# Redistributing weight-lookup steps between two phases of a fused attention and FFN kernel

## The chip, the core and the metric

The kernel runs as one program on one core of a Trainium2 chip. The metric is the device time of one execution in microseconds (us); the time before is the median of three runs. Engines are named as the profile names them: PE (TensorE matmul), PEld (its weight load), DVE (VectorE), ACT (ScalarE), POOL (GpSimd) and SP (SyncE, which issues most of the DMAs). PSUM is the memory that PE writes; SBUF is the memory that the other operands live in.

## What is computed

The input x has 8 sequences of 1024 tokens with 512 features. Cut to what matters, the reference is:

```python
xn = layernorm(x)
# recurrent attention, three decays i
q = xn @ Wq;  gate = softmax(xn @ Wg)
k = xn @ Wk[i];  v = xn @ Wv[i]
w = sigmoid(decay_logits[i]) ** max(s - t - 1, 0) * (s > t)
blended += gate[..., i] * ((q @ k.T * w) @ v)
s = blended @ Wo * out_scale
# FFN whose weights are looked up: w = lut[idx], lut has 16 entries
gate_ = xn @ lut[gate_idx].T;  up = xn @ lut[up_idx].T
h = silu(gate_) * up                                   # 1376 wide
g = silu(h @ lut[down_idx].T)
out = x + s * g
```

The FFN weights are not given; they are built on the chip from integer indices (1376x512, twice, and 512x1376) and a table of 16 floats.

## The kernel before

**Two phases.** `phase_1` runs the attention for all eight sequences, writes the blended result and the layer-normed inputs to DRAM, and beside that builds the FFN weights. `phase_2` runs the FFN for all eight sequences with matmuls in Winograd's form (products 1 to 7 of a 2x2 block scheme, nested twice), and ends with the multiplication of both parts.

**Lookups.** `look_up` (L212) builds one tile of weights, 128x1024, on DVE as a generator. Between two `yield`s stands one DVE instruction: three bit masks (`bit`, L217), one shift (L220), then a binary tree of eight `leaf` selections (L224) joined by seven `copy_predicated` (L241). One such instruction is called a lookup step here. When a tile is done, POOL adds and subtracts blocks of it (L271 to L275), and after every second tile it builds the tile `pair` (L289, L291, L296, L299 for gate and up; L335, L337, L340, L342 for down). Results go to DRAM through SP: L287, L297 and L300 for gate and up, L334, L338 and L343 for down, and L278 for those tiles (o of 8, 9 and 10) that are also needed whole. Stores are not issued at once: `defer(n, ...)` issues them after n calls of `tick`.

**Phase 1's loop.** For each b of 0 to 8 and each k of 0 to 7 (L741 onwards) three generators are advanced: `project(b)` (layer norm, transposes, features), `chunks(b - 1)` (the recurrence, one chunk of 128 tokens for each k) and `weights`, the build of FFN weights. One pass over k is called a slot here; in the trace a slot runs from one `pr` (L662) to the next. How many steps of `weights` a slot takes stands in the tuple `steps`, three places in a slot. Four slots are called a half.

In a slot DVE does, beside lookups, `pr` (L662, the masked scores that PE needs for `po`, L684), `ga` (L637, gate times query, which PE needs for the next slot's scores `psc`, L660), in some slots the sums `ts` (L515, L519, L524, L530) for the feature products, and twice an addition to `qk` (L537, L540). POOL does `qb` (L641) and small pieces of the layer norm (L423, L424).

The gates go a long way. After the softmax (L462) SP writes them transposed to DRAM (`gTd`, L468), and then reads them back for all partitions (`ga<-gTd`, L483); that read waits for the write. DVE's L637 reads what came back. Each b has two such trips, one per 512 tokens.

**Order.** `keep_order` chains each of PE, DVE, ACT and POOL to the order in which the program text issues them. SP is chained in that way only up to b of 0, k of 3; after that the recording layer places SP's DMAs, and SP works through them in that order: a DMA that waits holds up all behind it on SP.

**Phase 2's nodes.** `quads` (L960) goes through 17 nodes for each b. In a node PE does seven products; DVE makes `t[1] = t[1] + e` (L920) and `t[3] = t[2] + e` (L924), and product 3 cannot start before L920. In nodes (1, 1) and (5, 5) the results leave PSUM through ACT, in others through DVE. For b of 0, `left_weights` (L355) is advanced beside the nodes: one more tile of lookups, whose result (`wdl`) is needed after the last node. The line that does it before is

```python
                    some(made, 4 if node.ks in ((1, 1), (5, 5)) else 1)   # L1084
```

It stands after `node.seventh()`, so its DVE instructions follow L924 of the node and precede L920 of the next.

Of the kernel before, what the change touches and what calls it, by code (L numbers as in the profile page):

```python
# [48 lines left out]
def recurrent_block(ctx: ExitStack, tc, x, wq, wk, wv, wo, wg, decay_logits, out_scale, lut, gidx, uidx, didx, out):  # L49
# [19 lines left out]
    nc = tc.nc  # L69
# [13 lines left out]
    NQ = NO // 4  # L83
# [49 lines left out]
    def defer(parts, issue):  # L133
        later.append([parts, issue])
# [111 lines left out]
    def ffn_weights(build, pool, pair_pool):  # L246

        upper = []

        def gate_up(o):
            s, m = OCH[o]
            n = 2 * NV * m
            idx = build.tile([P, NB], I32, name="idx", tag="idx", bufs=2)  # L260
            iv = idx[:, :n].rearrange("p (a b) -> p a b", b=m)
            gs, us = (src[:, s : s + m].rearrange("(c p) b -> p c b", p=P) for src in (gidx, uidx))
            nc.sync.dma_start(out=iv[:, 2:6, :], in_=gs)
            nc.sync.dma_start(out=iv[:, 0:2, :], in_=us[:, 0:2, :])
            nc.sync.dma_start(out=iv[:, 6:8, :], in_=us[:, 2:4, :])
            yield
            wf = pool.tile([P, 2 * NB], F32, name="wgu", tag="wgu", bufs=3)
            yield from look_up(build, wf[:, :n], idx[:, :n], P, n)
            w = wf[:, : 2 * n].rearrange("p (k two m) -> p k two m", two=2, m=m)
            a21, a11, a12, a22, s1, s2, s3, s4 = (w[:, k] for k in range(8))  # L270
            nc.gpsimd.tensor_tensor(s1, a21, a22, ALU.add)  # L271
            nc.gpsimd.tensor_tensor(s2, s1, a11, ALU.subtract)
            yield
            nc.gpsimd.tensor_tensor(s3, a11, a21, ALU.subtract)
            nc.gpsimd.tensor_tensor(s4, a12, s2, ALU.subtract)  # L275
            wide = wf[:, 2 * m : 2 * n].rearrange("p (a b) -> p a b", b=m)
            if o >= 4 * NQ:
                defer(3, lambda: nc.sync.dma_start(out=wgu_d[o], in_=wide))  # L278
            if o >= 2 * NK:
                return  # L280
            if o % 2 == 0:
                upper.append(w[:, 1:])
                return
            up, low = upper.pop(), w[:, 1:]
            to = quad_d[o // 4][:, :, o // 2 % 2, :].rearrange("p k (t m) -> p k t m", m=P)
            pair = pair_pool.tile([P, 7, 3, P], F32, name="pair", tag="pair")
            nc.sync.dma_start(out=to[:, :, 0:2, :], in_=up)  # L287
            b21, b22, b11, b12 = low[:, :, 0], low[:, :, 1], up[:, :, 0], up[:, :, 1]
            nc.gpsimd.tensor_tensor(pair[:, :, 0], b21, b22, ALU.add)  # L289
            yield  # L290
            nc.gpsimd.tensor_tensor(pair[:, :, 1], pair[:, :, 0], b11, ALU.subtract)  # L291
            yield
            if o >= 4 * NQ:
                for _ in range(4):
                    yield
            nc.gpsimd.tensor_tensor(b21, b11, b21, ALU.subtract)  # L296
            defer(3, lambda: nc.sync.dma_start(out=to[:, :, 2:4, :], in_=low))  # L297
            yield
            nc.gpsimd.tensor_tensor(pair[:, :, 2], b12, pair[:, :, 1], ALU.subtract)  # L299
            defer(4, lambda: nc.sync.dma_start(out=to[:, :, 4:7, :], in_=pair))  # L300
            for _ in range(3):
                yield

        def down_tail():
            s, m = OCH[-1]
            idx = build.tile([P, NB], I32, name="idx", tag="idx", bufs=2)
            nc.sync.dma_start(out=idx[:m, :V], in_=didx[s : s + m, :])
            yield
            wf = pool.tile([P, 2 * NB], F32, name="wgu", tag="wgu", bufs=3)
            yield from look_up(build, wf[:m, :V], idx[:m, :V], m, V)  # L310
            defer(2, lambda: nc.sync.dma_start(out=wdt_d, in_=wf[:m, :V]))

        def down(rows, e):
            idx = build.tile([P, NB], I32, name="idx", tag="idx", bufs=2)
            for a, row in enumerate(rows):
                nc.sync.dma_start(out=idx[:, ts(a, V)], in_=didx[ts(row, P), :])
            yield
            t = pool.tile([P, 2 * NB], F32, name="wgu", tag="wgu", bufs=3)
            yield from look_up(build, t[:, : 2 * V], idx, P, 2 * V)
            b11, b12, b21, b22, t1, t2, t4 = (t[:, ts(k, V // 2)] for k in range(7))  # L320
            nc.gpsimd.tensor_tensor(t1, b12, b11, ALU.subtract)
            nc.gpsimd.tensor_tensor(t2, b22, t1, ALU.subtract)
            yield
            nc.gpsimd.tensor_tensor(b12, b22, b12, ALU.subtract)
            nc.gpsimd.tensor_tensor(t4, b21, t2, ALU.subtract)
            halves = t[:, : 7 * V // 2].rearrange("p (k o m) -> p k o m", o=2, m=P)
            if len(upper) == 0:
                upper.append(halves)
                return
            up, low = upper.pop(), halves  # L330
            b11, b12, b21, b22 = up[:, :, 0], up[:, :, 1], low[:, :, 0], low[:, :, 1]
            pair = pair_pool.tile([P, 7, 3, P], F32, name="pair", tag="pair")
            to = wd_d[:, :, e, :].rearrange("p k (t m) -> p k t m", m=P)
            defer(3, lambda: nc.sync.dma_start(out=to[:, :, 2:4, :], in_=low))  # L334
            nc.gpsimd.tensor_tensor(pair[:, :, 0], b12, b11, ALU.subtract)  # L335
            yield
            nc.gpsimd.tensor_tensor(b12, b22, b12, ALU.subtract)  # L337
            defer(2, lambda: nc.sync.dma_start(out=to[:, :, 0:2, :], in_=up))  # L338
            yield
            nc.gpsimd.tensor_tensor(pair[:, :, 1], b22, pair[:, :, 0], ALU.subtract)  # L340
            yield
            nc.gpsimd.tensor_tensor(pair[:, :, 2], b21, pair[:, :, 1], ALU.subtract)  # L342
            defer(4, lambda: nc.sync.dma_start(out=to[:, :, 4:7, :], in_=pair))  # L343
            for _ in range(8):
                yield

        jobs = [gate_up(o) for o in range(NO)] + [down_tail()]
        jobs += [down((j, j + 4), j % 2) for j in (0, 2, 1, 3)]
        next(jobs[0])
        yield  # L350
        for job, following in zip(jobs, jobs[1:] + [iter(())]):
            next(following, None)
            yield from job
# [347 lines left out]
    def phase_1():  # L701
        nonlocal small, p_a, p_c, p_r
        with (
# [37 lines left out]
            for b in range(B + 1):  # L741
                following = project(b + 1, pools, sides, kept) if b + 1 < B else iter(())
                older = chunks(b - 1, (chk, blp), kept) if b else iter(())
                for k in range(NC):


                    if b == 0:
                        steps = (k > 0, k >= NC // 2, 2 * (k >= NC // 2))
                    elif b < B:
                        steps = ((1, 1, 4), (1, 2, 4), (1, 2, 4), (1, 2, 3))[k % 4]  # L750
                    else:
                        steps = (1, 0, 0)
                    tick()
                    next(newer, None)

                    for _ in range((0, 0, 0, 0, 0, 0, 1, 2)[k] if b == 0 else k >= NC - 3):
                        next(following, None)
                    next(older, None)
                    next(setup, None)
                    build_some(steps[0])  # L760
                    next(more, None)
                    tick()
                    if k < NC // 2:
                        for _ in range(2):
                            next(ending, None)
                    next(newer, None)
                    build_some(steps[1])
                    next(older, None)
                    build_some(steps[2])
                    if k < NC // 2:  # L770
                        next(ending, None)
                    tick()
                    next(newer, None)
                    next(older, None)
                    if (b, k) == (0, 3):
                        sums_of_weights(wqk_sb, wqs)
                        keep_order(tc, seen, (mybir.EngineType.SP,))
# [16 lines left out]
    def phase_2():  # L794
        with (
# [164 lines left out]
            def quads(b, xs, h, sums, made, at_last):  # L960
# [108 lines left out]
                node, empty, after = next(todo)  # L1069
# [3 lines left out]
                while empty:  # L1073
# [7 lines left out]
                    at_last(node.ks == (2, 3))  # L1081
                    node.seventh()
                    empty(node.t, 3)
                    some(made, 4 if node.ks in ((1, 1), (5, 5)) else 1)  # L1084
                    node.product(1, 3)
                    empty(node.t, 1)
                    at_last(node.ks in ((5, 7), (2, 3)))
                    if following:
                        following.fifth()
# [10 lines left out]
            def some(weights, n):  # L1100
                for _ in range(n):
                    next(weights, None)
# [363 lines left out]
```

## Time and profile before

| | |
|---|---|
| median of three runs | 2103.63 us (2103.54 to 2104.08) |
| the profiled execution, its own time | 2103.83 us |
| its span, first to last instruction | 2101.9 us |
| PE busy | 2086.2 us, 99% |
| DVE, ACT, POOL busy | 1441.4, 943.6, 1038.5 us |
| phase 1 (until the first FFN product) | 0 to 584 us |
| lookups and their POOL work in phase 1 | until 539 us |
| `left_weights` in phase 2 | 584 to 678 us |
| mean granted TensorE clock | 0.999 |

The profile is one execution. Its page has the busy time of each engine, the span in 40 slices, the chain of work that ended last, and the costliest groups of instructions; further views list who waited for whom, the instructions of one engine in order of time, and busy time by stretch. In a line of the timeline the first number is the start in us from the begin of the span, the second the time, then engine, line, operation, what it writes and reads, and the count; a bracket gives idle time just before it and what ended it. Two instructions on one line (x2, x3) share the time. PE's matmuls overlap, so PE is bound where the next one starts a fixed time after the last: 216 ns for 256 columns. Where the start comes later than that, PE stood still.

### The profile page before, as it was taken

The page shows a single profiled execution, that of the slowest core. Times are in us where ns is not written, and L with a number is a line of the kernel's source. Part 1 is how long each engine was busy: PE and PEld are TensorE (multiplying, and loading weights), DVE is VectorE, ACT ScalarE, POOL GpSimd, SP SyncE. Part 2 cuts the span into 40 slices and gives each one's busy share as a digit, 9 for nine tenths or more (in the row PEclk, how much of TensorE's full clock was granted, in tenths as well). Part 3 has the DMA queues.
Part 4 walks back from the last instruction along what each step waited for, and adds up shares of the span by engine and source line. Part 5 has one row for each costly group of instructions (what it writes and reads, how often), then busy time and mean ns, then how long its engine had stood idle before and what let it go on. Part 6 is the DMA issues. An engine that isn't in the chain of part 4 may idle for free.

```text
span 2101.9 us, 32181 instructions
## 1 busy us (share of the span) xinstructions
PE 2086.2 (99%) x11691; PEld 1751.8 (83%) x11691; DVE 1441.4 (69%) x2214; ACT 943.6 (45%) x2116; POOL 1038.5 (49%) x1050
## 2 busy tenths in 40 slices
PE   9999999999999999999999999999999999999999
PEld 7887888888878888797878888787988888797877
DVE  8889998879357775675567456656755665675567
ACT  4766676676344324423531542344144224424531
POOL 4554664364364456517443741664275265527432
PEclk9999999999999999999999999999999999999999
DMA  8766769654754734554454446345544634464442
GB/s 218 147 178 165 208 149 211 158 164 125 210 177 139 258 134 161 169 216 145 157 215 152 160 151 238 138 149 196 189 146 153 249 128 158 151 233 145 146 156 106
DMA packets 184347, 359.68 MB, mean 171 GB/s; under 512 B 50895, under 2 KB 122206, under 8 KB 184190
## 3 DMA queue, kind: packets, MB, share of 16 engines
q1 hardware_dynamic: 168742, 330.61, 50.4%
q10 hardware_dynamic: 10968, 12.34, 1.8%
q0 software_dynamic: 4480, 14.68, 1.7%
q8 instruction: 93, 1.52, 0.3%
q14 instruction: 64, 0.52, 0.1%
HBM read 281.95 MB, written 75.63 MB: 170 GB/s over the span
## 4 chain that ended last, share of the span: by engine, by line
PE 81%; DVE 2%; DMA 1%; issue 0%; POOL 0%; ACT 0%; SPq 0%; DVEq 0%; ACTq 0%
PE s L897 33%; PE sE L897 6%; PE s12d L1154 5%; PE s21d L1154 5%; PE s11d L1154 5%; PE fs L845 3%; PE pd L1272 3%; PE ps L1279 3%; PE pv L444 2%; PE sEd L1154 2%; PE po L684 2%; PE fsE L845 1%; PE s11d L1165 1%; PE s12d L1165 1%; PE s21d L1165 1%; PE sEd L1165 1%
## 5 line engine op out<-in xcount | busy, mean ns | idle before, releaser
L897 PE MATMUL s<-xs,wq 128*128 128x256 f32 x3264 | 732.3, 380 | 2.3 <-DVE s L920 2.3
L897 PEld LDWEIGHTS s<-xs,wq 128*128 128x128 f32 x3264 | 620.0, 190 | 98.8 <-issue 8.4
L920 DVE TENSOR_TENSOR s<-s,e 128x512 f32<-128x512 f32 x136 | 95.1, 699 | 189.4 <-ACT s L919 189.4
L1243 POOL TENSOR_TENSOR cu<-cu 128x256 f32<-128x256 f32 x32 | 35.1, 1096 | 306.5 <-DVE cl L1242 306.5
L444 PE MATMUL pv<-wvg_sb,xnT 128*128 128x387 f32 x512 | 177.5, 488 | 0.2 <-DMA wvg_sb<-in_wv 0.2
L828 POOL TENSOR_TENSOR xs<-xs 128x256 f32<-128x256 f32 x224 | 171.8, 793 | 6.8 <-PE fs L845 2.3
L924 DVE TENSOR_TENSOR sE<-s,e 128x512 f32<-128x512 f32 x136 | 95.1, 699 | 104.0 <-PE s L897 104.0
L990 POOL TENSOR_TENSOR u<-u,e 128x512 f32<-128x512 f32 x64 | 80.4, 1278 | 134.1 <-DVE u L986 101.9
L915 ACT COPY e<-sE 128x512 f32<-128x512 f32 x136 | 79.6, 585 | 142.5 <-PE sE L897 142.5
L897 PE MATMUL sE<-xs,wq 128*128 128x256 f32 x544 | 140.5, 381 | 0.0
L444 PEld LDWEIGHTS pv<-wvg_sb,xnT 128*128 128x128 f32 x512 | 94.2, 190 | 54.1 <-issue 0.4
L994 POOL TENSOR_TENSOR h<-h,u 128x512 f32<-128x512 f32 x64 | 81.1, 1287 | 110.2 <-DVE u L1001 110.2
L423 POOL TENSOR_SCALAR rstd<-rstd 128x1 f32<-128x1 f32 x56 | 26.6, 475 | 205.9 <-ACT junk L422 204.8
L908 ACT COPY s<-s 128x512 f32<-128x512 f32 x136 | 77.5, 570 | 109.6 <-PE s L897 106.2
L919 ACT COPY s<-s 128x512 f32<-128x512 f32 x136 | 77.5, 570 | 97.8 <-PE s L897 97.8
L1154 PE MATMUL s12d<-wdd,z 128*128 128x128 f32 x896 | 118.4, 275 | 0.6 <-ACT s12d L1176 0.6
L897 PEld LDWEIGHTS sE<-xs,wq 128*128 128x128 f32 x544 | 104.0, 191 | 14.3
L1154 PEld LDWEIGHTS s12d<-wdd,z 128*128 128x128 f32 x896 | 109.0, 192 | 0.8 <-ACT s12d L1176 0.8
L224 DVE TENSOR_SCALAR leaf<-idx,lut_x,lut_sb 128x1024 int32<-128x1024 int32 (+2 forms) x119 | 108.2, 933 | 0.0
L641 POOL TENSOR_TENSOR qb<-ga,q_tab 128x384 f32<-128x384 f32 x56 | 77.1, 1377 | 55.5 <-DVE ga L637 37.8
L241 DVE COPY_PREDICATED leaf<-bit,leaf 128x1024 f32<-128x1024 uint8 (+2 forms) x68 | 93.0, 1368 | 1.7
L1283 POOL TENSOR_TENSOR gx<-gx,cu 128x512 f32<-128x512 f32 x32 | 40.8, 1278 | 82.0 <-DVE cu L1281 64.5
(266 smaller groups left out, 4517.3 us busy)
## 6 DMA issues: line engine op xcount, KB each, us to landing
wq<-quadd SPq DMA_DIRECT2D x112, 896.0 KB, 4.5
wdd<-wdd SPq DMA_DIRECT2D x56, 896.0 KB, 4.7
xs<-xsd SPq DMA_DIRECT2D x56, 512.0 KB, 6.5
wq<-quadd SPq DMA_DIRECT2D x48, 448.0 KB, 4.0
x<-in_x SPq DMA_DIRECT2D x64, 256.0 KB, 6.4
xsd<-ts SPq DMA_DIRECT2D x16, 1024.0 KB, 12.8
gx<-in_x SPq DMA_DIRECT2D x64, 256.0 KB, 6.1
out<-gx POOLq DMA_DIRECT2D x56, 256.0 KB, 2.3
```

The lines of the kernel that those rows point to most:

```text
L224: nc.vector.tensor_scalar(o.bitcast(I32), iv, lut_x[:rows, k, :], lut_i[:rows, k, 0:1], ALU.bitwise_and, ALU.bitwise_xor,)
L241: nc.vector.copy_predicated(o, bits[level - 1][:rows, :n], t[:rows, :n])
L444: nc.tensor.matmul(pv, lhsT=xnT[:, v, ts(c, P)], rhs=wvg_sb[:, v, :], start=(v == 0), stop=(v == NV - 1))
L828: nc.gpsimd.tensor_tensor(o, x1, x2, ALU.subtract)
L845: nc.tensor.matmul(ps, lhsT=w[:, 2 * W_OF[k] + n, :m], rhs=xs[:, X_OF[k], 2 * n : 2 * n + 2, :], start=start and n == 0, stop=stop and n == 1,
L897: nc.tensor.matmul(self.t[n][:, ts(a, H)], lhsT=self.w[:, a, (0, 1, 6, 3, 4, 5, 2)[i - 1], :], rhs=self.xs[:, X_OF[self.ks[a]], D_OF[i], : ...
L920: nc.vector.tensor_tensor(self.t[1], self.t[1], self.e, ALU.add)
L924: nc.vector.tensor_tensor(self.t[3], self.t[2], self.e, ALU.add)
L990: nc.gpsimd.tensor_tensor(o[:, n], o[:, n], other[:, n], ALU.add)
L994: nc.gpsimd.tensor_tensor(of_h(half, n), of_h(half, n), two(other[:, n]), ALU.mult)
L1154: nc.tensor.matmul(self.t[n][:, ts(a, P)], lhsT=self.lhs[i][:, e, ts(a, P)], rhs=self.w[:, e, D_OF[i], :], start=start and a == 0 and e == ...
L1165: nc.tensor.matmul(self.t[n][:, ts(a, P)], lhsT=self.left[:, ts(2 * (n // 2) + a, P)], rhs=wd_left[:, D_OF[self.k], ts(n % 2, P)], start=F ...
```

## The change

There are four edits. In phase 1, the first slot of a half takes three steps at its third place instead of four. In phase 2, nodes (1, 1) and (5, 5) advance `left_weights` twice instead of four times at the first place, and a second place after product 3 takes one step in (1, 1) and two in (5, 5). For the tiles that are also stored whole (o of 8 or 9), the four blank steps in front of the subtraction that overwrites part of the tile (L296) are gone; instead the generator yields until the store's issue has been recorded in `left`.

```diff
             wide = wf[:, 2 * m : 2 * n].rearrange("p (a b) -> p a b", b=m)
+            left = []
             if o >= 4 * NQ:
-                defer(3, lambda: nc.sync.dma_start(out=wgu_d[o], in_=wide))
+                defer(3, lambda: left.append(nc.sync.dma_start(out=wgu_d[o], in_=wide)))
...
-            if o >= 4 * NQ:
-                for _ in range(4):
-                    yield
+            while o >= 4 * NQ and not left:
+                yield
             nc.gpsimd.tensor_tensor(b21, b11, b21, ALU.subtract)
...
-                        steps = ((1, 1, 4), (1, 2, 4), (1, 2, 4), (1, 2, 3))[k % 4]
+                        steps = ((1, 1, 3), (1, 2, 4), (1, 2, 4), (1, 2, 3))[k % 4]
...
-                    some(made, 4 if node.ks in ((1, 1), (5, 5)) else 1)
+                    some(made, 2 if node.ks in ((1, 1), (5, 5)) else 1)
                     node.product(1, 3)
                     empty(node.t, 1)
+                    some(made, (node.ks == (1, 1)) + 2 * (node.ks == (5, 5)))
```

No instruction is added or removed; the order of instructions on DVE, POOL and SP changes from b of 1 onwards. NQ is 2, so o of 8 and 9 are the paired tiles that the wait concerns, and only o of 9 reaches the line.

## The prediction

> **What bounds the kernel now.** I read the page first, then PE's own waits, then the engines' timelines around each place where PE stood still.
>
> ```profile
> span 2101.9 us, 32181 instructions
> PE 2086.2 (99%) x11691; PEld 1751.8 (83%) x11691; DVE 1441.4 (69%) x2214; ACT 943.6 (45%) x2116; POOL 1038.5 (49%) x1050
> ```
>
> PE leaves 15.7 us idle, and the change adds no matmul and takes none away. So every other engine matters only where it lets PE stand. PE's waits name the places:
>
> ```profile
> PE po L684 <- DVE pr L662: 2.5, 3, 1.4
> PE s L897 <- DVE s L920: 2.3, 1, 2.3
> PE pe L505 <- DVE ts L515: 1.6, 3, 0.8
> ```
>
> All three end with DVE, the engine whose queue the change re-orders. These waits leave out short gaps, so I also compared each matmul's start with the usual spacing (112 ns for 128 columns, 216 for 256, 327 for 387). In phase 1 after the warm-up this finds 1.53 us at 98.0, 1.57 in 116 to 122, 2.11 in 172 to 195, 0.73 at 226, 0.28 at 267, 0.65 at 376: together 6.87. In phase 2 there is one place, at 650 (below). Start-up, 573 to 584 and 708 to 720 hold the rest, which the change does not reach.
>
> **Phase 2, node (1, 1) of the second group.** The timeline of all engines:
>
> ```profile
> 644.47 6.87 POOL L994 TENSOR_TENSOR h<-h,e 128x512 f32<-128x512 f32 x4
> 644.88 3.07 DVE L224 TENSOR_SCALAR leaf<-idx,lut_x,lut_sb 128x1024 int32<-128x1024 int32 x2
> ...
> 647.99 2.26 DVE L241 COPY_PREDICATED leaf<-bit,leaf 128x1024 f32<-128x1024 uint8 x1
> ...
> 650.15 1.74 DVE L224 TENSOR_SCALAR leaf<-idx,lut_x,lut_sb 128x1024 int32<-128x1024 int32 x1
> 651.81 0.69 DVE L920 TENSOR_TENSOR s<-s,e 128x512 f32<-128x512 f32 x1
> ...
> 652.55 1.75 PE L897 MATMUL s<-xs,wq 128*128 128x256 f32 x4 [2.27 <-DVE s L920]
> ```
>
> Four steps take 6.9 us beside POOL (alone a leaf takes 0.81, a copy 1.31), L920 is late, PE wanted to start at 650.12. The next 3.4 us of matmuls come 427 ns apart instead of 216: the granted clock of the stretch 650 to 700 is 0.97, half speed for 3.4 us. Gap and slow clock cost 2.43 + 1.74 = 4.17.
>
> The edit does less here than it seems: the empties of (1, 1) are on ACT, so no DVE instruction lies between the two places. What counts is that (1, 1) takes three steps, not four. In the changed order they are copy, leaf, leaf. Against before one leaf of 1.66 (start to start) is gone, so L920 ends at 650.9 and PE stands 0.8. Gaps of 1.53 (at 98) and 1.0 us (at 194) were not followed by half clock, so I take none. Gain 4.17 - 0.87 = 3.3. Node (5, 5) still gets four in a row, now leaf, leaf, copy, copy, 4.24 alone, for which the room is about 4.5; its successor gets a copy beside POOL's L990. I charge 0.2 for these. Sum **-3.1**, from -4.2 (no gap left) to -1.5 (half clock stays).
>
> [...]
>
> **Phase 1, lag of DVE.** A slot of PE is 7.1 to 9.5 us. DVE falls behind where a slot's lookups and POOL's operations meet:
>
> ```profile
> 85.42 7.59 DVE L217 TENSOR_SCALAR bit<-idx 128x1024 uint8<-128x1024 uint8 x3
> ...
> 97.75 1.30 DVE L241 COPY_PREDICATED wgu<-bit,leaf 128x1024 f32<-128x1024 uint8 x1
> 98.94 0.55 DVE L662 TENSOR_TENSOR pr<-psc,w_tab 128x384 f32<-128x384 f32 x1
> ```
>
> Three bits take 7.59 beside the pair operations (L291 to L299, 2.5 each), where one alone takes 0.69. `pr` comes 6.5 after its scores, PE can bear 5.0, gap 1.5. I laid the changed order of DVE and POOL, slot by slot, over durations from this trace (0.73 a leaf, 1.2 a copy, 0.6 a bit, start to start; 2.5 for each one that meets a pair operation; 0.7 a slot for `qb`). In this slot one copy (1.2), one leaf (0.7) and one more step's share go: `pr` starts some 2.6 earlier, no gap. Each half has one step less, about 1 us, so the lag no longer adds up: `pr` is 1 to 3.9 late, where 3.4 to 5.8 can be borne. Narrow remain the slot at 113 (`ts` 0.4 late) and that at 259 (0.2). The gap at 376 came from late gates (below), and goes because that gate write now precedes the stores; in exchange L296 waits there for the whole store to land (0.3 for a late `qb`). Of 6.87 some 0.9 stay: **-6.0**, from -6.9 to -3.5.
>
> **The end of phase 1: a new wait.** Fewer steps per half and a later start of each tile move the last lookup from slot 53 to slot 55: its copy ended at 526.0, now at about 545.7 (`qk` at 535.06 holds two leaves back, then slot 55 has 8.6 of work). POOL's eight operations follow. They took 13.1 then (526.05 to 539.05, one `qb` of 1.0 among them); now 12.1 and about 1.6 of meetings with DVE's L637, L462 and sums: until 559.4. SP then issues the store of `pair` (L343), and in the changed order of SP the last gate write, L468, stands directly behind it. Before, L343 was 13 us ahead and the write waited only for the softmax:
>
> ```profile
> 553.72 0.36 SPq L468 DMA_DIRECT2D gTd<-g  x1
> ...
> 565.05 0.33 SPq L483 DMA_DIRECT2D ga<-gTd  x1
> ```
>
> What a gate write behind a pair's store costs, this trace shows at b of 5:
>
> ```profile
> 347.57 0.53 SPq L297 DMA_DIRECT2D quadd<-wgu  x1
> 348.19 0.61 SPq L468 DMA_DIRECT2D gTd<-g  x1
> ...
> 361.59 0.33 SPq L483 DMA_DIRECT2D ga<-gTd  x1
> ```
>
> ```profile
> 366.38 0.56 DVE L662 TENSOR_TENSOR pr<-psc,w_tab 128x384 f32<-128x384 f32 x1 [0.24 <-PE psc L660]
> 371.47 0.56 DVE L637 TENSOR_TENSOR ga<-ga,qk 128x384 f32<-128x384 f32 x1 [4.54 <-DMA ga<-gTd]
> ```
>
> There the write waited from 342.6 (softmax done) for POOL, took 13.4, the read 9.8, and PE lost 0.65, because three long slots cover 29 us. After the last write the slots are short (5.8, 6.5, 6.5): L637 used the gates at 570.69, and PE's scores stand at 572.35. Now: write issued at 560.2, 13.4 to the read's issue (10.3 to 14.6 over all of them), 7 for the read (5.1 behind little, 9.8 behind much), 0.6 for L637: 581.2. PE is late by 8.85, some 1 us of it already at `qb`, which stands behind L342 on POOL. A gap that long brings half clock, 1.65 more as at 650. Sum **+10.5**, from +4 to +15. Queued behind the write on SP are the input sums' store and the loads of `xs` (needed at 584), which have PE's own delay to land in. The write before it, at 487, gets the same neighbour (L343 at about 485) but has long slots; I charge nothing, and 2 us if its read takes 9.8.
>
> **Sum.** -3.1 - 6.0 + 10.5 = +1.4 against the profiled execution's 2103.83 (its span plus 1.9 outside); the median is 0.2 lower, so 2103.63 + 1.4 = **2105.0**.
>
> **Rivals.** About 0.2% (4.2 us) is what a measurement here can tell from no change.
> - The parts cancel to within 4.2: likeliest, 0.50. Its own range is 2099.5 to 2107.8.
> - The late gate write costs little (last copy earlier, or a write of 10.3 and a read of 5.1 behind a store that is already through: +3 to +4). For it: the rows 524.16 to 534.75, and that the trace has shown 6.87 + 4.17 of gaps to gain. Against it: the write cannot pass L343 on SP, nor L343 the pair operation. Then -9 + 3 gives 2097.5, at best 2095. 0.22.
> - Slower: the same write, with the read at 9.8 because it queues behind 1.3 MB of `pair` and 1 MB of sums, and the restart at half clock. From a landing at 571.7 on PE waits one to one; from 583.4 on the cost is over 13.3 and outweighs the gains of 9.1 by more than 4.2. Price 14 to 16: 2108.5 to 2110.5; it is the same if phase 1 keeps half its gaps. 0.28.
> - That the change does nothing in phase 1 would need the same order; the order differs on DVE, POOL and SP from b of 1, so I give it no share.
>
> **Numbers.** Forecast 2105.0; range 2095.5 to 2111.0, which takes in most of both outer cases. Faster 0.22, within 0.50, slower 0.28.
>
> **What would show it.** Right, if PE's waits no longer have `s` <- L920 above 1 us, and no clock of 0.97 at 650; if the gap at 98 is under 0.5; if L468 near 560 follows L343 and L637 near 580 shows a wait for `ga<-gTd` of 8 to 10, with PE idle at `psc` and half clock after it. Wrong, if the last copy of phase 1 ends before 540, if the last gates land by 572, or if phase 1 has new gaps over 1 us at `pr`.

## The result, and the profile after

| | before | after |
|---|---|---|
| median of six runs each | 2102.64 us (2101.22 to 2104.08) | 2114.15 us (2112.01 to 2114.51) |
| the profiled execution | 2103.83 us | 2112.01 us |

The change makes the kernel slower: ratio 1.0053, 95% interval 1.0040 to 1.0066. The forecast was 2105.0, its range ended at 2111.0. The profiled execution of after is the quickest of its six, 2.1 below the median, and that of before lies 1.2 above its median. So what is read from the two traces accounts for 8.2 of the 11.5 us between the medians. For the rest there is the mean granted clock that is on record for each execution of after: 0.997 for the two at 2112.01 and 2112.99, 0.996 for the four from 2114.01 on. One more stretch of 3.4 us at half clock lowers the mean by 0.0008 and costs 1.7 us (an estimate from the stretches in these traces), so it would be most of the 2.1. Where it would lie no trace shows.

From the page of after, the busy times (its span is 2110.0 us):

```profile
PE 2087.3 (99%) x11691; PEld 1754.0 (83%) x11691; DVE 1452.7 (69%) x2214; ACT 943.8 (45%) x2116; POOL 1036.1 (49%) x1050
```

PE's matmuls are as many as before, so the 8.1 us of span are time in which PE stood or ran at half clock. PE's waits (for whom, us in total, times, longest):

```profile
PE psc L660 <- DVE ga L637: 6.8, 1, 6.8
PE po L684 <- POOL qb L641: 4.2, 2, 2.9
...
PE po L684 <- DVE pr L662: 1.1, 1, 1.1
PE s L897 <- DVE s L920: 0.6, 1, 0.6
```

The last line is the one in phase 2 that stood at 2.3 before. The first two are new. Busy time and granted clock (PEclk, third from the end) by stretch show where PE ran slow: 0.97 of 60 us and 0.93 of 50 us are one and two stretches of 3.4 us at half clock.

```profile
340.00:400.00 60.00, 57.11 (x322) 47.97 (x321) 38.64 (x58) 41.14 (x109) 27.94 (x28) 0.97 0.72 168
540.00:590.00 50.00, 41.95 (x278) 38.58 (x277) 29.43 (x47) 13.30 (x38) 21.34 (x15) 0.93 0.78 207
```

**A ledger for all runs.** For every matmul I took the time to the next one's start, less the usual spacing for its number of columns, and summed by stretch. The sums hold gaps and slow clock together; a stretch without any comes out slightly negative. The last column is the whole span; what lies between 400 and 550 (-0.6) and behind 700 (0.4, in `turn2_second` 0.7) has no column. All values in us, one profiled execution each; the kernels are told below.

| stretch | 0-60 | 60-340 | 340-400 | 550-600 | 600-700 | all |
|---|---|---|---|---|---|---|
| before | 2.9 | 5.6 | 0.4 | 1.4 | 4.2 | 14.1 |
| after | 2.6 | 3.3 | 4.6 | 11.1 | 1.0 | 22.2 |
| p2 | 3.2 | 5.7 | -0.3 | 1.4 | 1.2 | 11.0 |
| steps | 2.7 | 2.8 | -0.3 | 10.2 | 4.3 | 19.4 |
| left | 2.8 | 5.5 | -0.3 | 1.4 | 4.5 | 13.7 |
| act | 2.7 | 2.6 | 2.7 | 6.8 | 0.9 | 15.5 |
| store_act | 2.5 | 8.2 | 0.4 | 10.1 | 0.9 | 21.9 |
| turn | 2.5 | 3.3 | 1.9 | 2.8 | 0.8 | 11.1 |
| turn_store | 2.9 | 7.4 | -0.1 | 3.1 | 0.9 | 14.0 |
| early | 3.1 | 7.3 | 6.5 | 1.3 | 0.9 | 18.9 |
| turn2 | 2.9 | 3.1 | 0.6 | 3.3 | 0.8 | 10.5 |
| shift | 2.6 | 9.4 | -0.3 | 1.4 | 0.9 | 13.9 |
| second | 2.6 | 3.0 | 5.6 | 10.7 | 0.9 | 22.5 |
| turn2_second | 2.6 | 2.7 | 1.0 | 3.2 | 0.8 | 10.5 |

After minus before is 8.1, as the spans say. Two places lose: 340 to 400 (+4.2) and 550 to 600 (+9.7). Two gain: 60 to 340 (-2.2) and phase 2 (-3.2). The start-up differs by 0.3.

**The place at 366.** Before, SP issues the whole store of tile 9 when its data are ready (337.99), ahead of the gate write at 348.19, and POOL's L296 hardly waits for it:

```profile
338.02 0.33 SPq L278 DMA_DIRECT2D wgud<-wgu  x1
...
345.46 2.08 POOL L296 TENSOR_TENSOR wgu<-wgu 128x896 f32<-128x896 f32 x1 [0.29 <-DMA wgud<-wgu]
```

After, in the timeline of all engines:

```profile
343.01 0.38 SPq L468 DMA_DIRECT2D gTd<-g  x1
...
349.54 0.73 POOL L275 TENSOR_TENSOR wgu<-wgu 128x256 f32<-128x256 f32 x1
...
354.75 0.33 SPq L483 DMA_DIRECT2D ga<-gTd  x1
...
355.17 0.38 SPq L279 DMA_DIRECT2D wgud<-wgu  x1
...
364.26 2.08 POOL L296 TENSOR_TENSOR wgu<-wgu 128x896 f32<-128x896 f32 x1 [6.88 <-DMA wgud<-wgu]
...
368.65 1.30 POOL L641 TENSOR_TENSOR qb<-ga,q_tab 128x384 f32<-128x384 f32 x1
...
370.00 1.28 PE L684 MATMUL po<-qb,R 128*128 128x128 f32 x6 [2.89 <-POOL qb L641]
```

Read it upwards. PE waits for `qb`; `qb` stands on POOL behind L296 and L299 (366.30 to 368.69); L296 overwrites part of tile 9 and waits until the whole store of that tile (L279, L278 before) has landed; the store had its data at 350.3 (the end of L275) but stands on SP behind the read of the gates, and that read waits 11.7 for the gate write to land. A lookup's store is late because of an attention gate.

**The end of phase 1.** The same view:

```profile
558.80 2.46 POOL L342 TENSOR_TENSOR pair<-wgu,pair 128x896 f32<-128x896 f32 x1
...
561.28 0.51 SPq L343 DMA_DIRECT2D wdd<-pair  x1
561.88 0.61 SPq L468 DMA_DIRECT2D gTd<-g  x1
...
576.62 0.33 SPq L483 DMA_DIRECT2D ga<-gTd  x1
...
581.82 0.56 DVE L637 TENSOR_TENSOR ga<-ga,qk 128x384 f32<-128x384 f32 x1 [7.86 <-DMA ga<-gTd]
...
582.48 0.77 PE L660 MATMUL psc<-ga,qk 128*128 128x128 f32 x2 [6.77 <-DVE ga L637]
```

The last gate write is ready at 556.1 (softmax, L462) and goes out at 561.88, directly behind the store of `pair`, for which L342 ended at 561.26; 14.7 to the read's issue, 5.2 to L637.

### The profile page after: what moved, and what is told of

Its sections match the earlier page's. It is cut to its first block, busy times and chain, and to the rows that moved or that the text cites. A ratio compares the mean times of both kernels' runs of the same rounds, so it can differ in the third digit from the quotient of the medians.

```text
span 2110.0 us, 32176 instructions
## 1 busy us (share of the span) xinstructions
PE 2087.3 (99%) x11691; PEld 1754.0 (83%) x11691; DVE 1452.7 (69%) x2214; ACT 943.8 (45%) x2116; POOL 1036.1 (49%) x1050
## 4 chain that ended last, share of the span: by engine, by line
PE 92%; DVE 4%; DMA 2%; issue 1%; POOL 1%; ACT 0%; SPq 0%; DVEq 0%; ACTq 0%; POOLq 0%
PE s L897 33%; PE pv L444 7%; PE sE L897 6%; PE s12d L1155 5%; PE s21d L1155 5%; PE s11d L1155 5%; PE fs L845 3%; PE po L684 3%; PE pd L1273 3%; PE ps L1280 3%; PE sEd L1155 2%; PE pa L505 2%; PE pe L505 2%; PE pc L505 2%; PE psc L660 2%; DMA gTd<-g 1%
## 5 line engine op out<-in xcount | busy, mean ns | idle before, releaser
L920 DVE TENSOR_TENSOR s<-s,e 128x512 f32<-128x512 f32 x136 | 95.1, 700 | 190.0 <-ACT s L919 189.9
L444 PE MATMUL pv<-wvg_sb,xnT 128*128 128x387 f32 x512 | 177.4, 488 | 0.0
L444 PEld LDWEIGHTS pv<-wvg_sb,xnT 128*128 128x128 f32 x512 | 94.2, 190 | 53.7
L897 PEld LDWEIGHTS sE<-xs,wq 128*128 128x128 f32 x544 | 103.4, 190 | 14.1
L994 POOL TENSOR_TENSOR h<-h,e 128x512 f32<-128x512 f32 x64 | 81.1, 1302 | 0.0
## 6 DMA issues: line engine op xcount, KB each, us to landing
xsd<-ts SPq DMA_DIRECT2D x16, 1024.0 KB, 13.2
```

The costliest lines, as they stand in the source:

```text
L444: nc.tensor.matmul(pv, lhsT=xnT[:, v, ts(c, P)], rhs=wvg_sb[:, v, :], start=(v == 0), stop=(v == NV - 1))
L897: nc.tensor.matmul(self.t[n][:, ts(a, H)], lhsT=self.w[:, a, (0, 1, 6, 3, 4, 5, 2)[i - 1], :], rhs=self.xs[:, X_OF[self.ks[a]], D_OF[i], : ...
L920: nc.vector.tensor_tensor(self.t[1], self.t[1], self.e, ALU.add)
L994: nc.gpsimd.tensor_tensor(of_h(half, n), of_h(half, n), two(other[:, n]), ALU.mult)
```

## The experiments

My theory at the start: four separate places, of which the edit of the step counts causes both losses. The rivals stand with each run. The kernel before was run beside each: its medians are 2102.7 beside p2, steps, left and act, 2102.7 beside store_act, turn, turn_store and early, 2103.5 beside turn2, shift and second, 2103.4 beside turn2_second. The ratios are to these.

**One part at a time.** `p2` is the kernel before with the edit in phase 2, `steps` with `(1, 1, 3)`, `left` with the wait for the store's issue.

p2: 

> The kernel before with the edit in phase 2 alone. Theory: the four edits act at separate places, and this one takes the gap at 650 and the half clock behind it: 3.3 us faster than before (2.5 to 4.2), no half clock after 640, phase 1 as before. Rival: the gain in phase 2 exists only because phase 1 ended later, which shifted the clock's windows; then the gap shrinks but half clock stays and the gain is 1.6 or less.

Measured 2100.55 (2099.76 to 2102.03), ratio 0.9989, interval 0.9980 to 0.9997. In the ledger 600 to 700 falls by 3.0 and nothing else moves by more than 0.7. PE's wait for L920 that was 2.3 is now 1.0, and the granted clock of the stretch 640 to 700 is 1.00. The gain in phase 2 stands by itself; the rival falls. The medians show 2.1, less than the 2.5 expected at least. The profiled executions are 3.3 apart, but that of before is among its longer ones: of the 29 executions of before beside this run, all 13 from 2103.3 on have a mean granted clock of 0.999, and of the 16 below that 13 have 1.000. So the half clock that the traced execution shows at 650 seems to be missing from many others, and there is less to gain in them; only one execution of before has a trace, so the place is not shown.

steps: 

> The kernel before with three steps in place of four in the first slot of a half, and nothing else. Theory: all that the change lost comes from this edit, the place at 366 too, since the order of POOL and SP around L296 is that of the changed kernel without the edit of the wait: 4 more at 366, 9.7 more at 575, 2.6 less before 340: 10 to 13 us slower than before. Rival: the loss at 366 belongs to the wait for the store's issue; then this kernel loses at 575 alone and is 6 to 8 slower.

Measured 2109.39 (2108.73 to 2109.84), ratio 1.0031, interval 1.0019 to 1.0042. Half of my theory falls, and the rival's 6 to 8 comes true: the end loses 8.8, nearly as in after, but at 366 there is no gap. The timeline of POOL and SP shows why:

```profile
356.90 2.08 POOL L296 TENSOR_TENSOR wgu<-wgu 128x896 f32<-128x896 f32 x1
...
359.01 0.32 SPq L278 DMA_DIRECT2D wgud<-wgu  x1
```

The store comes after L296, not before it. With the step counts changed, the four blank steps are over before the store's turn has come, so L296 has nothing to wait for, and the store writes tile 9 after the subtraction has overwritten half of it; what this kernel reads back for product 4 of that tile is, in that half, the difference and not the tile. So the wait edit belongs to the step edit: it keeps the right data, and the 4.8 us at 366 (after against `steps` in the ledger, before rounding) are what keeping them costs in that place.

left: 

> The kernel before with the wait for the store's issue in place of the four blank steps, and nothing else. Theory: the blank steps and the wait take about the same number of steps; within 1.5 us of before, POOL's L296 waits for the store about 0.3 to 2 us where nobody is kept. Rival: the wait is what puts L296 behind a store that has not landed; then PE loses 3 to 5 at 345 to 370 and the kernel is 3 to 5 slower.

Measured 2103.36 (2101.87 to 2104.05), ratio 1.0000, interval 0.9991 to 1.0009. Alone the edit is worth nothing, as the theory had it: with the old step counts the store is issued early. The sum of the three single runs is -2.1 + 6.7 + 0.7 = 5.3 against 11.5 for all; 4.8 of the 6.2 between them are the place at 366, which needs two edits at once.

**The last gate write.** In `act` ACT issues it, in place of SP; in `turn` PE transposes the gates and ACT writes them in 12 rows of 512 bytes, as the kernel does for one trip of b of 0.

```diff
-                    nc.sync.dma_start(out=there.rearrange("k p -> p k"), ...)
+                    queue = nc.scalar if (b, hf) == (B - 1, 0) else nc.sync
+                    queue.dma_start(out=there.rearrange("k p -> p k"), ...)
```

act: 

> The changed kernel with the last gate write (b of 7, hf of 0) issued by ACT, so that it no longer stands behind the store of the pair on SP. Theory: the loss at 575 is the place of the write on SP; the write then starts near 553, lands near 565, the read is back by 572, and 8 to 10 of the 11 us of lost time between 550 and 600 go: 2104 to 2106.5, that is 1.5 to 4 slower than before. Rival: the read itself is late because it shares the queues with the store of the pair and the sums; then it takes 9 to 10, the scores wait 3 to 5 us all the same, and only 3 to 5 are gained: 2109 to 2111.

Measured 2108.04 (2105.19 to 2110.49), ratio 1.0024, interval 1.0015 to 1.0033; expected 2104 to 2106.5. The timeline of ACT, SP and DVE (from L469 on this kernel's lines stand one further down):

```profile
553.83 0.43 ACTq L469 DMA_DIRECT2D gTd<-g  x1
...
567.06 0.34 SPq L484 DMA_DIRECT2D ga<-gTd  x1
...
574.76 0.56 DVE L638 TENSOR_TENSOR ga<-ga,qk 128x384 f32<-128x384 f32 x1 [3.29 <-DMA ga<-gTd]
```

The write starts 8 us earlier but still takes 13.2; the read takes 7.7 more. PE waits 2.4 instead of 6.9. So the place on SP is one part of the loss, the slow element-wise write another.

```diff
-            if (b, hf) == (0, 1):
+            if (b, hf) in ((0, 1), (B - 1, 0)):
                 defer(3, turn)
```

turn: 

> The changed kernel with the last gates (b of 7, hf of 0) transposed on PE and written by ACT in rows, as the kernel does it for b of 0, hf of 1, in place of the element-wise write on SP. Theory: the end of phase 1 is late because the write is late and slow (13 us), not because the read is; the read can be issued right behind the store of the pair at 561.3 to 563 and is back at 568 to 571, so the wait of the scores goes but for 1 us and with it both windows of half clock: 8 to 9.5 faster than the changed kernel, 2104.5 to 2106.5. Rival: the read is held up by the store of the pair; then the gates are back at 573 or later, 3 us of wait and one window of half clock stay, and the gain is 4 to 6.

Measured 2104.66 (2100.87 to 2106.01), ratio 1.0008, interval 0.9999 to 1.0016: 9.5 faster than after, as expected. The trace is of an execution of 2100.94, with no half clock.

```profile
555.11 0.32 ACTq L476 DMA_DIRECT2D gTd<-gs  x1
...
559.90 1.29 SPq L483 DMA_DIRECT2D ga<-gTd  x1
...
571.18 0.55 DVE L637 TENSOR_TENSOR ga<-ga,qk 128x384 f32<-128x384 f32 x1
```

The write has landed 4.8 after its issue at the latest, though a store of the down weights (L338, issued at 553.46) runs beside it as in `act`; L637 has no wait. The loss at the end is the late and slow write, not the read. Both runs issue the write on ACT, and the same 6 KB took 13.2 word by word and at most 4.8 in rows.

**The store of tile 9.** `store_act` is after with the whole stores issued by ACT (`defer(2, lambda: left.append(nc.scalar.dma_start(...)))`); `turn_store` is that and `turn`.

store_act: 

> The changed kernel with the whole stores of tiles 8 to 10 issued by ACT, two ticks after the subtraction, so that the store of tile 9 no longer stands on SP behind the read of the gates. Theory: L296's wait of 6.9 at 364 is the place of that store on SP; it then starts near 353 instead of 355.2, L296 follows some 2 us earlier, the gap at 366 shrinks from 3.05 to about 1 and its half clock goes: 3.5 to 4.7 us faster than the changed kernel, 2109.5 to 2111. Rival: the 9.1 that the store takes are not its place but its neighbours on the DMA engines; then it takes longer by what it starts earlier and less than 1 us is gained.

Measured 2112.91 (2111.52 to 2118.64), ratio 1.0057, interval 1.0043 to 1.0071: 1.2 below after, within the two kernels' spread; expected 2109.5 to 2111. The gap at 366 is gone, another has come in its place:

```profile
321.58 0.33 ACTq L279 DMA_DIRECT2D wgud<-wgu  x1
321.95 0.59 ACT L438 COPY xnT<-pt 128x512 f32<-128x512 f32 x1 [3.91 <-DVE ga L637]
...
322.59 2.05 PE L444 MATMUL pv<-wvg_sb,xnT 128*128 128x387 f32 x3 [3.19 <-ACT xnT L438]
```

On ACT the copy `xnT` (321.95) stands behind the store of tile 8 (321.58). PE waits 3.4 for that copy and runs at half clock: the eight matmuls of L444 from 322.59 on take 4.56, where in after eight of them from 346.39 on take 2.77. The store's data were ready at 319.32 (the end of POOL's L275), so POOL is not what holds it. What came last ahead of its issue is the landing, at 321.48, of another store (`xsd<-ts`, L531, issued by SP at 309.48), which the trace has on the same DMA semaphore; no run here tests whether that is the reason. Neither theory had that. On SP, in after, the same store went out at 320.88 without a cost to PE. Nor is the gap at 366 gone by what was meant: L296 still waits 4.1 for the store of tile 9 and starts at 366.42, 2.2 later than in after, but PE comes to this place 4.9 later, by the new gap and its half clock, and `qb` (done at 371.85) is just in time.

turn_store: 

> Both: the changed kernel with the last gates through PE and with the whole stores on ACT. Theory: the two losses are independent, so both gains add up: 12 to 14 faster than the changed kernel, 2100 to 2102.5, that is 0 to 2.5 faster than before; what is left are the gaps at 114, 120, 263, 559 and 650. Rival: the window of half clock comes back at another place; then 2102.5 to 2105.

Measured 2104.98 (2103.24 to 2110.22), ratio 1.0012, interval 1.0003 to 1.0021: no better than `turn` alone, with the same new gap at 319 (ledger 60 to 340: 7.4). The theory's 2100 to 2102.5 is missed; the rival's figure comes true, by this gap and its half clock.

`early` takes three steps only while b is below 3 and has the stores on ACT (`(1, 1, 3 if b < 3 else 4)`).

early: 

> The changed kernel with three steps in a half's first slot only for b of 1 and 2 and four after that, and with the whole stores on ACT. Theory: the gaps that the fewer steps removed lie at 98 and at 172 to 195 (b of 1 and 2), while the late end comes from the steps left out later; with four of eleven late steps only, the last subtraction for the pair ends near 550, the last gate write is not kept, and the loss at 575 goes: 2098.5 to 2101.5, faster than before by 1 to 4. Rival: half a slot of delay is enough for the store of the pair to hold the gate write again; then 2104 to 2109.

Measured 2108.18 (2105.15 to 2110.42), ratio 1.0026, interval 1.0016 to 1.0036. The end is healed (1.3 in the ledger: L343 goes out at 549.71, the last gate write at 561.79). But at 366 L296 waits 8.4 for a store that takes 13.1 to land, and the gap is 3.9 with half clock behind it. Right for the end, wrong for the whole: the rival's figure comes true by another cause. This store was not behind the read on SP: ACT issued it at 347.79, 1.5 after its data were ready, so what made L296 late is mainly its landing.

**The cause at 366, taken away.** `turn2` is after with two trips through PE: the last, and that of b of 4, hf of 0, whose read holds SP in front of the store (`(b, hf) in ((0, 1), (4, 0), (B - 1, 0))`).

turn2: 

> The changed kernel with two gate trips through PE and rows in place of the element-wise write: the last one (b of 7, hf of 0) and the one of b of 4, hf of 0, whose read stands on SP ahead of the whole store of tile 9. Theory: L296's wait at 364 comes from that read, which holds SP for the 11.7 that the element-wise write takes; with a quick write the store is issued as soon as its data are there (350.3 in the changed kernel), L296 ends its wait by 360, the second product's operand is in time and gap and half clock at 366 go: 3.5 to 4.8 faster than the kernel with the last trip alone changed (2104.66), that is 2100 to 2101.5. Rival: the store lands late because of its neighbours, as the two runs with the stores on ACT hint (7.1 and 13.1 to land); then half of the gap stays and less than 2 us is gained.

Measured 2101.07 (2100.50 to 2102.30), ratio 0.9989, interval 0.9980 to 0.9998: 13.1 faster than after, and faster than before. SP and POOL:

```profile
350.56 0.33 SPq L279 DMA_DIRECT2D wgud<-wgu  x1
...
358.07 2.36 POOL L296 TENSOR_TENSOR wgu<-wgu 128x896 f32<-128x896 f32 x1
```

The store is issued when its data are there (the read of the gates follows at 350.99), L296 has no wait, PE none at 366. The theory holds as far as the gate trip goes: with the slow write gone, the loss is gone. But two things changed at once. The store goes out when it is ready and not 4.9 later, and it lands in 4.5 us and not in 9.1. In after L296 would have had to start by 361.2 for PE not to wait (364.26 less the 3.05). By these numbers either change alone would have done: 350.3 + 9.1 is 359.4, 355.2 + 4.5 is 359.7. That is an estimate; no run separates them, and what sets the landing time of this store (4.5 here, 7.1 in `store_act`, 9.1 in after, 13.1 in `early`) stays open.

**The lag before 340.** `shift` makes up at b of 3 and 4 what b of 1 and 2 leave out, so that DVE's order from b of 5 on is the old one (`4 - (b < 3)` in the first slot, `3 + (2 < b < 5)` in the last); `second` takes the step out of the second slot (`((1, 1, 4), (1, 2, 3), ...)`), and `turn2_second` is that with the two trips.

shift: 

> The changed kernel with the steps that are left out at b of 1 and 2 made up at b of 3 and 4 (four in the last slot of a half instead of three) and four in the first slot from b of 3 on, so that from b of 5 on each instruction of DVE stands where it stood before the change. Theory: the losses at 366 and 575 are a matter of where lookups stand from b of 5 on, and the gains at 98 and 172 to 195 of where they stand at b of 1 and 2: both losses go, both gains stay, and the gain in phase 2 too: 2098 to 2100.5, that is 2 to 4.5 faster than before. Rival: the lag comes back at b of 3 and 4 with 27 steps in a half; then 2101 to 2103.

Measured 2103.41 (2102.89 to 2103.88), ratio 1.0000, interval 0.9991 to 1.0009. Both losses are gone, as expected. But the steps put back at b of 3 and 4 bring gaps of 1.7 at 230, 1.2 at 265 and 1.9 at 299, larger than any that before has in these places: 9.4 between 60 and 340, where before has 5.6. The rival is right in its cause, and 0.4 above its figure; a step does not go for nothing into any slot.

second: 

> The changed kernel with the step taken out of a half's second slot (three in place of four at its third place) instead of its first. Theory: DVE's lag follows from which lookup steps meet POOL's operations in a slot, not from their number in a half; the gap at 98 comes back (1 to 1.5), that at 114 shrinks, and those at 366 and 575 stay, since the total is the same: 2113 to 2116. Rival: the number in a half decides; then the gaps before 340 are those of the changed kernel and nothing moves by more than 0.5 us at any of them.

Measured 2112.40 (2112.13 to 2112.87), ratio 1.0043, interval 1.0031 to 1.0056. Neither side. The gap at 98 stays away (so a step less in either slot does for it), while 114 falls from 1.3 to 0.6 and 263 from 1.0 to 0.3, and 242 gains 0.6 (so these follow the slot).

turn2_second: 

> The kernel with two gate trips through PE, and in it the step taken out of a half's second slot instead of its first. Theory: the places are independent, so the gaps before 340 are those of the kernel with the second slot (about 0.6 us less at 114 and 0.7 less at 263, 0.6 more at 242) and those at 366 and 575 stay away: 0.4 to 1 faster than the kernel with the two trips (2101.07), 2100 to 2100.8. Rival: the two added transposes on PE meet the later step and stand there for DVE; then 2101 to 2102.

Measured 2100.59 (2099.82 to 2101.32), ratio 0.9987, interval 0.9978 to 0.9996: as expected, the lowest median of those tried that have the step edit, if not clear of `turn2`'s, and no better than `p2`, which leaves phase 1 alone.

## Why the prediction was wrong, step by step

It had four places, and had the sign of three; at 366 it expected a small gain and there was a loss. Predicted were +1.4, the traces show +8.1. The median of after lies 9.1 above the forecast: 6.7 of that are the terms below, 2.1 the distance of after's median from its traced execution.

| term | predicted | trace |
|---|---|---|
| phase 2, node (1, 1) | -3.1 | -3.2 |
| lag of DVE before 340 (in the trace with 0.3 of start-up) | -5.65 | -2.5 |
| the place at 366 | -0.35 | +4.2 |
| end of phase 1 | +10.5 | +9.7 |

- **Phase 2: right**, in size and by its reason. A gap of 0.8 was forecast, 0.80 is there (at 661), and no half clock. The size is that against the traced execution of before; between the medians `p2` has 2.1.
- **The place at 366: the step that failed most**, 4.5 of the 6.7. The prediction said "in exchange L296 waits there for the whole store to land (0.3 for a late `qb`)". The wait was named and priced next to nothing, and what it waits for was not followed up: the price has no place for a store that SP issues late. In front of it on SP stands the read of the gates, which waits for a write of 11.7. The store left 4.9 after its data were ready, landed 9.1 later, and PE lost 3.05 and 1.7 more by half clock. `turn2` shows that the loss goes with the slow write, `steps` that it exists only because L296 has to respect the store. The other half of this term, the gap of 0.65 at 376 that was to go because the gate write precedes the stores, is gone in after; but it is also missing from the traces of `p2` and `left`, whose order of gate write and stores is the old one, so the reason is not shown.
- **The lag: mis-sized**, 3.2 of the 6.7. "Narrow remain the slot at 113 (`ts` 0.4 late) and that at 259 (0.2)": they measure 1.3 at 114 (at `pr`) and 0.9 at 120 (at `ts`), and 1.0 at 263 (at `ts`). For `pr` the prediction had "1 to 3.9 late, where 3.4 to 5.8 can be borne"; at 114 it starts 4.7 after its scores (110.83), and PE could bear 3.4. Before:

```profile
115.99 0.83 PE L684 MATMUL po<-qb,R 128*128 128x128 f32 x6
116.15 0.55 DVE L662 TENSOR_TENSOR pr<-psc,w_tab 128x384 f32<-128x384 f32 x1
```

  After:

```profile
114.11 0.83 PE L684 MATMUL po<-qb,R 128*128 128x128 f32 x6
...
115.48 0.55 DVE L662 TENSOR_TENSOR pr<-psc,w_tab 128x384 f32<-128x384 f32 x1
```

  Because the gap of 1.5 at 98 is gone, PE comes to this slot 1.9 earlier, DVE only 0.7. So most of what was gained at 98 is lost again at 114: a gap that closes takes room from the slots behind it. At 120 another thing adds to it. The layout stretched DVE only where it meets the 896-wide pair operations, but POOL's 256-wide ones (L271 to L275, 115.67 to 119.67) do it too: two bits from 115.94 take 2.14 where the layout had 1.2, and `ga` at 118.00 takes 1.08 where it takes 0.55 alone. What makes DVE late at 263 stays open. The gaps at 98 and 172 to 195 went as predicted. Which rule says in what slot a step is free is not settled: `second` and `shift` show that both the number and the place count.
- **End of phase 1: right** in mechanism and nearly in size, the latter in part by luck, as errors cancel. The last copy ended at 547.6 (545.7 predicted), the write took 14.7 (13.4), the read with L637's wait 5.2 (7); PE wanted its scores at 575.5 and not at 572.35, because more had been lost and less gained ahead of it. Half clock came for 6827 ns (578.64 to 585.47), not for 3413; up to 582.48 it lay inside the gap and cost nothing.
- **The rivals.** "The late gate write costs little" is out. "Slower" had 0.28, at 2108.5 to 2110.5; its reason (a read of 9.8) did not come true, its clause "the same if phase 1 keeps half its gaps" did, and 366 came on top.
- **The signs.** Of the prediction's own signs those of being right came, the wait for `ga<-gTd` with 7.9 a little below its 8 to 10; but one of being wrong came too, a new gap over 1 us at `pr`, that at 114.
- **The chances** put half on a sum of large terms cancelling within 4.2, while one of the two added waits had been looked at only at its own end.

## What to carry to other kernels

Where a change makes an operation wait for a store, price the store's place in its queue as well as its transfer: ask what the entry in front of it waits for, and take its landing time as a range (here 4.5 to 13.1 us for the same 896 KB). Look for a DMA that depends on another DMA and has a third behind it in its queue: here the read of the gates went out on SP 11.7 us after the gate write that it waited for, and 4.9 of them fell on the store behind it. A gap that closes brings the engine earlier to the next place, so ask there anew what can be borne. And where one step is moved to make room, look for the shared resource that now sees a different neighbour at the other end of the program; here steps left out from b of 1 on put the last store of a pair on the wrong side of a gate write some 460 us later.

## What the runs showed of the hardware

**The length of a gap alone did not tell whether half clock followed.** In the traces of before and after the slow stretches, at a granted clock of 0.50, last 3413 ns or twice that, but for the one that begins at the very end of the program. In each of the two their starts lie whole multiples of 3413.3 ns apart: in after they are at 370.43, 578.64 and 2107.81 (61 and 509 times that behind the first), in before at 652.93 and 2100.18 (424 times). For six gaps I measured what share of the 3413 ns right ahead of the slow stretch PE stood idle:

| run, gap | length, us | idle share of the 3413 ns ahead | half clock behind it |
|---|---|---|---|
| before, 650 | 2.43 | 0.71 | yes |
| act, 573 | 2.36 | 0.68 | yes |
| early, 364 | 3.89 | 0.62 | yes |
| after, 367 | 3.05 | 0.88 | yes |
| act, 366 | 2.85 | | no |
| after, 575 | 6.93 | 0.91 | yes, 6827 ns |

A gap of 2.85 was followed by none and cost nothing more; one of 2.36 was, and that cost 1.7. Counted back from the slow stretch of `act` in steps of 3413 ns, one step ends inside its gap of 2.85, which leaves PE idle for 0.56 of that step and 0.27 of the next. That this is why no half clock followed is my reading; no run tests it. The times of one kernel spread with the mean granted clock on record: in `turn` it is 1.000 at 2100.87 and 2100.94, 0.999 for the eight from 2102.88 to 2104.92, 0.998 at 2106.01; in `act` it goes from 0.999 at 2105.19 to 0.997 at 2110.49. One stretch is worth 0.0008 and 1.7 us (the estimate above, from 3413 ns at half clock), so half clock is part of the spread and not all of it. Those executions have no trace, so at which gap it came is not shown.

**A small write took longer here than a large load.** The gate writes of 1536 words of four bytes (L468) took 10.2 to 14.7 us to land in the traces of before, after, `turn` and `turn2`, where the 896 KB loads of phase 2 (`wq<-quadd`) land in 4.5, the median on the pages of before and after.
